# Nine unread products of ones around the transposes of the first tile's second norm, in a two-layer recurrent kernel

## Chip, cores and metric

One Trainium2 chip, one core. The metric is the device time of the kernel in microseconds (us). Most executions of a kernel agree within 0.3%. The engines are called by their short names: PE (TensorE: PE its products, PEld its weight loads), DVE (VectorE), ACT (ScalarE), POOL (GpSimd) and SP (SyncE, whose queue issues nearly all DMAs).

## What is computed

32 sequences of 256 tokens with 128 features go through two layers. Each layer normalizes its input, computes a recurrent branch `s` and a gate branch `g`, and adds `s * g`:

```python
x = L0_attn_x                                   # (32, 256, 128)
xn = _layernorm(x, axis=-1)
s = _L0_attn_ref(xn, ...)                       # k, v, r; decayed sums of exp(k) and exp(k)*v; sigmoid(r); Wo
g = _silu(_L0_ffn_ref(xn, ...))                 # three products with matrices of +1 and -1, relu between
x = x + s * g
xn = _layernorm(x, axis=-1)                     # the second norm
s = _L1_attn_ref(xn, ...)                       # W_in, causal conv of 4, silu, W_x, W_dt, softplus, a scan, W_out
g = _silu(_L1_ffn_ref(xn, ...))                 # 2 shared and 16 routed experts, the 4 likeliest, gelu
x = x + s * g
```

## The kernel before

The tokens are cut into 16 tiles of 512 (two sequences), numbered 0 to 15. Most of a tile's arrays are 128 features x 512 tokens. A product that must be exact in float32 is made of three products of rounded parts ("h" for the high part, "l" for the low one: w_h by x_h, w_l by x_h, w_h by x_l, the helper `mm3`, recorded at L634); each moves 512 columns. The products of seven of the nine expert groups (`pm<-act,w_n`) and the transposes are in plain float32.

Each stage of a tile is a Python generator that issues one instruction per step: `norm0`, `part0`, `mix`, `sign0` to `sign2` (tiles pha, phb, pz), `key`, `kv`, `recept` (pk, pv, pr), the sums, `quot`, `back` (po, and the transposes pt back to tokens x features), `norm1` (psb), `conv`, `proj`, `logits`, `router`, `gates`, `res`, `decay`, `gain`, `scan`, `outp`, `up`, `weigh`, `down`, `gate1`, `end`. What stands between two generators' steps is set by hand over the whole kernel: `ORDER` is a text of three-character entries, a tile and a stage, and the instruction that the stage issues next is put there. So every engine's queue is a part of one written list, and each engine works through its own part in that order. `SLOTS` names, for each buffer a stage asks for, which of the pool's places it gets; "psq" is the eight PSUM banks.

The place of the change is the second norm of tile 0. `norm1` takes statistics of the four 128-token pieces of `pt` on DVE (bsb, mvb: L659, L664), the inverse root on POOL (mvb, L669), normalizes each piece on DVE into `xnb` (L952, one 128x128 instruction per piece), and transposes each on PE into one bank `psb` (L956). ACT then copies the bank to x20h (L959, rounded) and DVE takes the rest x20l. All that follows in the second layer reads these two: the products pi and pres (`conv`, `res`), pl (`logits`, eight products of 32 columns, then DVE's reduction L1027) and pu (`up`, nine groups). The router goes on with an exponential of lg on ACT, and further reductions on DVE.

ACT evaluates its functions from tables. The helper `act` issues a table load (L410) where the function at hand isn't in the set that was loaded last. A kind "G" is the set with gelu, "S" the one with silu, "E" the one with exp and ln, "P" softplus. `tr` (tanh, in `recept`) is in "S" and in "G", and loads "S" where neither is there.

Products of ones are in the kernel already: `warm` (L493, L498) fills `wm`, 128x256, with ones, and issues WARM = 14 products `wm[:, 0:P]` by `wm` of 256 columns into a bank that nobody reads, 10 of them ahead of everything else on PE and four among the first products.

Of the kernel before, what the change touches and what calls it, by code (L numbers as in the profile page):

```python
# [16 lines left out]
P = 128  # L17
# [34 lines left out]
WARM = 14  # L52
WV = (1,)
# [54 lines left out]
        '0123045678250312530171120573663507222367502257603220367566275301132570002713511573207735201330152711'  # L108
        '357206635027117026535263170'
# [6 lines left out]
        '0123401221043210301243011043210424013240043210433104231001324103031423011023410220143201120341021204'  # L116
        '3120102341022103421001243103'
    ),
    'h': (
        '012341056789abc5147603ac167459b82def9f2d5fe89417cb6a30gd48ac84d7g23b9f51915fb193604827gdca4cag8c54d7'  # L120
        '2063bf9171736190afb42d8g5cb8b248c5gd71a963f07d63d7g849b25c0fa1b99c5b48d3f6g71a02a20172ag639fd85c4be4'
        'f3c53f90ga21674ff47624fa8b19g05c3e1b1c5b2697f48ae30gdb3d0ed345g8f679c18c96cba817f05dg416'
# [9 lines left out]
        '0123410532610762151760432154257262016421360403546030127013755147531650250435453743502615376542325635'  # L132
        '5753521073136243242133567061627674711474103462732241025402151603761476713733521354075716274030762700'
        '4561460135170171251324756562403123012105370657246247120643475127161340041041556237265737431704011604'
        '2056241673213723576060417245472522043734110723756356236247104323156315753653271534161721672027526342'
        '6405161501767261530175276374267743035134723640622474501664673701272140251706307130235045041507620543'
        '7316236723023754745104604303663025467375102130252312413657025302164301037637441270463527141026134571'
        '0012572743160732457347563'
    ),
    'rest': '0000000000000000',  # L140
    'rs': '01101010101010100101100110010110',
# [3 lines left out]
        '0120201210331200456721389046509183462920504382631594807461390470825a23481018973273991307128628531064'  # L145
        'a15037951a05430697341a87260489a3b0b63649623b0961257a3498c6892a756c68657a60b836a79543a584b890a3589c20'
        'b7240b5373b025053b78a504a2b580738b403a7283c9c4a09538c4537907c389405a6943ca2b65c4539b6935c2ab53c9b738'
        'a4c9057ba9874830b4a97b33b0296875920b657b989075a842b7653c1616c518474b42714812b0220021847b58451058501b'
# [4 lines left out]
    'xi': '01101010011001100110011010010110',  # L153
    'xna': '00',
    'xr': '0123454012354012',
# [5 lines left out]
g0pg0pg0pg0pg0p000g0hg0fg0pg0fg0fg0fg0fg00g0fg07g08g01100g0pg03002002002g0pg0fg0fg0gg0gg0hg04002g0og0o002g0g002002002g0g  # L161
g0g002g0ig0i002002002102102102g0jg0j102102102102102102g02g0gg0ag09g0cg0fg0fg0fg0m002g0k002002g0b002002102002002200002g0q
g0f102004g0fg0mg0d003008005102g0q102004102g0j003g0l005008004g0eg0kg0og05g0kg0fg0f102004102102006006102102102005300g0vg06
005007007008g0j00800e00e00e10100g00g00600g00e009006g0j00e00900900700700e00f00fg0j10300i00i00i00i00a00a00a00a00a00a00900a
00a00a10300900900900920220220220220220210510500g201g0v00f20220200b00b00b00b00900900h301g0l40100140000cg0t00cg0t20200c00c
00c00c00c20200c00j10600h106g0u00j00b00a00b00b00b00h202g0l00j00bg0r00b00j10820220200cg0u00cg0r10510510710720200d00dg0tg0t
g0t108g0sg0t109109106202302g0s10700j00d00d00d30210400j10c00d30210810c00d30250030230230230230210400j00d00k30200j00l00l109
10600l40210a30210c40220200l00l10c30210730210910430210a10410a10910810cg0ng0n10910c50240210e10e40270040240240240230200l00l
00l50240210c00m00l00m10c10c10e00m00m00m00m00m00m00m10i10i10e00m10910910a50250260040210a50250250250210a10a10a10e00m50210e
10a00m00m00m00m00m00m00m00m00n10f10f20210i109g0n50200m10f20400n00o20300n30210j10900q00n00q10c00q00q00q00q00q00o00q01s01s  # L170
01s10j60200q00n20360200o01k60201k00q60201k80060260200q60260201100r01s10j60201101101860210i00r00n01801800r00r00r30201k00n
01o01c00r00r01c70201o00r00r10a01100r01801c01o01470200r01410g01100r10g01o00r00r01gg0ng0n10g00o01110b01c01400r00r00n00o01g
01g70200u70200r10g10b01410b70270270270270200u00r01g90000u70210b00o00t00t10h00t10d01510b00n01901d00o10b00n10b10h00n10b10d
10d10d01l00u01p01w00o10b01001w10h01w01000o00o00o10b01001001030310d10d01601310d10d10j00t10j00p01601h01630401a00p00p10k00p
01301380201e01701720620680200p10j01080201t01780210j01x00p01ma0001b20610j10l10l20401q10l10l00s00z00z00z00s00s00w01f00w10l
00v20420820601i00v00z00z10l00z00y00y10l10l01u20880210l80280280201w10m10m20701j20700y10m20710m20520500x00x10m10m10m20501n
01y10m10m01020801r01v20701020801z10m20502040201020i20410m20i20e20940240280290200x80210m10m40220920e90210m10m20i20i10m10m
20e90210m40220920e10m20c90220910m902902902902209209c0010o10n20e10o10n00z90220c902a0210n00za02a02a0220e00z10q10qb0010q10q
10q10q30320f10q20f10q20f10o10n20950102120910o20a20a20c40210o20a02110n10q10q10q10n20j10r20j02102120c40220c20c20c10r10r20c
02102120c20a11802120a20911820j40311802111811120c11111111c10r20911c11c11c40411k10r10o10r10r20a40311k02111o11o11k10r11o10r  # L180
11k10r10o20a20a10r11o10r11g11110r11g11g10r11s10r10n11g11s11s10r10o11411411120g20g10r20g20a11111410r11s20b10n11420b20b115
20g10t20b11d20b20a20b20b20h11310n10n10n20b11911320h20b11l10t10t10u10u10u20h20b20d20d20d20d20d11610o10o10z10z10z10o11311t
10t11p20j11e10p11620j10u11w10p10p20j10p20d20d11w20d10p11611h20j11a11x11w20k11711711011020j20l20l20l10p11m11711w20l305305
30810s11b30530420l10s10s10z10w308305110110110a02a02a02a0211q10w30420l10v10y10y11i10v20l20l20l30e11f30820m30e20m30630610y
10x10x10z11y11010z50230811j50250230620m11u110502307307307a0230611n50220m20m20m20m20m20m11011r30720m11011vb0230420mb02b02
b0211z10x120a0220m20m30id0030i30930i30920m20m60120m20m20m30i30e30930e30a30a10z30e40410z10z30e30f30f20m50230c40430a30f30a
30930930c30930930c30c30c30930c12150230930c30c12120n20m12112120n30j12112130c20n30920o30c30j20o20n20o30a12120n20q20q20q20q
20q20q20q12120q21120o20q21121120q30j20o30a20q21k30a30a20n20r20r20r20r21k12140421o21o21k21s20r21c21k20o21s21s21o21121c21c
20o21s21g21c20r21g20r21820r20r20n20r21821121821420r21821420r20r21g20r21421130a30g30g21g30g20r21o30b30a20r30b30b20o20r214
30b30b30g30b20r21w21321w30b20n30h21321320o20o20t21520t20t30h20o21w21d20n20n30b30d30h20n21930d21l20t30d30d30j21t30j21030b  # L190
21030b30j20u50450330d20u20u21021021030d30d30j21630d21e21020u21h30j30l30l21630k40640621a21p30l30l40620z21x20z20z21640620p
21720p20p20p21720z20z30l20p21721b21m30l20p21i30l30l21u20s30l30m30m20w30m30m21f21j20s20s20w21q30m30m30m30m30m20y20y20v405
40520v21n21r30mc02c02405c0240521w40720y20x40760220x21y21v602602407b02602b02b02b02408c0240i40i20z210e0040821z40i407b02b02
21030m22060221040i20x40e70140930m30m40e40e30m30m30m30m40930m20z40840c40940e50430m30m20z20z40a40a40e40e60240c40c409408409
40940c40940c40c22122160240c40f40f40c40f40a40940c40a30o40922130o50422122122130n22150440j40a30n40j30n40940c30n30q30q30q221
30q30q30q30q30q30o40a40a30q30n40a30q30q30o30r40j30n30r30r30r31850322131c31c31831831c31131831131130n31k30o30r31o31o31o31c
31130r30r31k31k31k30r30r30n30r31s31s31s30r30r31430r30r31430o31431131g31o31g30r31g31131s40g40g40a30r40g30r30o31w31w31g40a
30r31w31440b40b40g40b40b31530o40b40b40b30t30n30n40b31d30n30t31331930t31l31330o30o40h30o31p31340d40h40d40d40d40b40h40j30u
30t30u40b30u60330p31630p30p31h40j40j31630p50650630p40d40d31e40d31731640d40j31730u31031040j40k31a31t31x40l40l60430p40l40l
31050631031050631m30z30z31740l30s30z30v30s30s30w31i31b30w30vc02c02c02c0240l30y30y30z30z31f40l40l31w40m31u40m70240l30z702  # L200
# [96 lines left out]
def recurrent_d2(  # L297
# [634 lines left out]
    def norm1(i):  # L932
# [3 lines left out]
        if N1 == "b" and i not in N1D:  # L936
            yield from spread(s, "xn2", mv, f"b{i}", lambda: s["r"], "back", E1)
            yield
            nc.scalar.copy(hi_of(s, "x2", f"x2{i}", "x2"), s["xn2"])
            yield  # L940
            lo_of(s, "x2", f"x2{i}", "x2", s["xn2"], E1[2])
            return
        for j in range(NJ):
            yield
            if j == 0:
# [437 lines left out]
```

## Time and profile before

| what | value |
|---|---|
| median of 3 runs | 659.92 us (659.65, 659.92, 661.74) |
| the profiled execution, its own time | 659.82 us |
| its span from the first to the last instruction | 658.0 us |
| mean granted clock of PE over the span | 0.993 |
| ACT's table loads (L410) | 99, 127.0 us in all, 1283 ns each |
| the transposes of the second norms (L956) | 64, in tile 0 from 39.54 us |

The page gives each engine's busy time, cuts the span in 40 slices of 16.45 us, and follows back the chain of work that ended last. Timelines give start, duration, engine, line, operation, tiles, and in brackets the idle time before with what ended it. A busy PE is not PE at its peak, since products overlap: how far apart they begin says more than how long each lasts. Times in a timeline or window are us from the start of the span.

### The profile page before, as it was taken

How to read it: one execution, taken by the hardware profiler on the slowest of the kernel's cores; microseconds unless marked ns; L12 is line 12 of the kernel's file. 1: busy time of each engine (PE TensorE's matmuls, PEld its weight loads, DVE VectorE, ACT ScalarE, POOL GpSimd, SP SyncE). 2: the span in 40 equal slices, each digit the busy share in tenths (PEclk: the TensorE clock that was granted, in tenths of full speed). 3: DMA queues.
4: the chain of work that ended last, by engine and by line, in shares of the span. 5: the costliest groups of instructions: out<-in, count | busy, mean ns of one | idle time of the engine just before them, and what ended most of it. 6: DMA issues, size and time to landing. Idle time of an engine off the chain costs nothing.

```text
span 658.0 us, 8819 instructions
## 1 busy us (share of the span) xinstructions
PE 641.4 (97%) x2626; PEld 461.5 (70%) x2626; DVE 572.2 (87%) x1364; ACT 549.3 (83%) x911; POOL 384.0 (58%) x398
## 2 busy tenths in 40 slices
PE   8999999999999999999999999999999999999997
PEld 6667676876757777576777767677675876767664
DVE  5989999979988899888888988988888798979886
ACT  8969797878969879797888979889797997967984
POOL 6585848567392773828466393944738374262542
PEclk9979999999999999999999999999999999999999
DMA  7334223142230413204132220413123040310431
GB/s 239 138 80 142 69 84 113 64 130 65 93 103 32 137 59 114 65 24 144 43 132 65 87 91 30 133 49 130 47 71 110 17 130 12 91 46 0 146 94 69
DMA packets 43648, 57.38 MB, mean 87 GB/s; under 512 B 3936, under 2 KB 20432, under 8 KB 43600
## 3 DMA queue, kind: packets, MB, share of 16 engines
q1 hardware_dynamic: 43456, 56.80, 26.9%
q8 instruction: 21, 0.34, 0.2%
q14 instruction: 27, 0.22, 0.1%
q10 hardware_dynamic: 144, 0.01, 0.0%
HBM read 52.02 MB, written 4.78 MB: 86 GB/s over the span
## 4 chain that ended last, share of the span: by engine, by line
PE 78%; DVE 11%; ACT 6%; issue 2%; DMA 2%; POOL 1%; SPq 0%; DVEq 0%; ACTq 0%
PE phb L634 15%; PE pm L634 14%; PE pu L634 13%; PE pc L634 6%; PE pha L634 4%; PE pz L634 3%; PE pi L634 3%; PE py L634 3%; PE pres L634 3%; PE pp L634 2%; PE po L634 2%; PE pk L634 2%; PE pl L634 2%; PE pv L634 1%; ACT L410 1%
## 5 line engine op out<-in xcount | busy, mean ns | idle before, releaser
L414 POOL TENSOR_TENSOR act<-act,ge 128x512 f32<-128x512 f32 x109 | 139.2, 1301 | 19.3 <-DMA ge<-gd 14.7
L410 ACT ACT_TABLE_LOAD x99 | 127.0, 1283 | 2.8 <-PEq L1371 1.2
L634 PE MATMUL pm<-act,w_n 128*128 128x512 f32 x224 | 106.0, 592 | 0.0
L417 DVE SCALAR_TENSOR_TENSOR pi<-xiz,par_sb,pi 128x512 f32<-128x512 f32 x96 | 70.4, 744 | 1.0 <-ACT pi L976 0.7
L414 POOL TENSOR_TENSOR xc_0l<-y,xc_0h 128x512 fp32r<-128x512 f32 x15 | 19.4, 1296 | 85.0 <-ACT y L411 64.3
L634 PEld LDWEIGHTS pm<-act,w_n 128*128 128x128 f32 x224 | 41.8, 189 | 29.9 <-issue 23.5
L411 ACT ACTIVATE act<-pu 128x512 f32<-128x512 f32 x109 | 61.2, 601 | 1.2 <-PE pu L634 0.3
L414 POOL TENSOR_TENSOR y<-y,rs 128x512 f32<-128x512 f32 x30 | 38.3, 1278 | 18.7 <-DVE y L1122 18.1
L1122 DVE TENSOR_TENSOR_SCAN y<-pd,y 128x256 f32<-128x256 f32 x64 | 39.9, 669 | 4.4 <-ACT pd L411 4.1
L414 POOL TENSOR_TENSOR xr<-gm,xr 128x512 f32<-128x512 f32 x15 | 19.3, 1288 | 30.1 <-DVE gm L414 25.1
L634 PE MATMUL phb<-ha_0h,w 128*128 128x512 f32 x64 | 27.3, 431 | 0.1
L1056 POOL MEMSET m<- 128x16 f32 x16 | 1.8, 112 | 43.7 <-DVE m L1054 43.7
L634 PE MATMUL phb<-ha_0l,w 128*128 128x512 f32 x64 | 26.1, 410 | 0.0
L634 PE MATMUL phb<-ha_2h,w 128*128 128x512 f32 x64 | 25.6, 403 | 0.0
L634 PE MATMUL phb<-ha_1h,w 128*128 128x512 f32 x64 | 25.5, 401 | 0.0
L634 PE MATMUL phb<-ha_3h,w 128*128 128x512 f32 x64 | 25.5, 398 | 0.0
L411 ACT ACTIVATE pd<-pd 128x512 f32<-128x512 f32 x32 | 17.9, 581 | 9.0 <-PE pd L634 8.8
L634 PE MATMUL phb<-ha_3l,w 128*128 128x512 f32 x64 | 25.3, 396 | 0.0
L634 PE MATMUL phb<-ha_2l,w 128*128 128x512 f32 x64 | 25.2, 397 | 0.0
L952 DVE TENSOR_SCALAR xnb<-pt,mvb 128x128 f32<-128x128 f32 x64 | 22.8, 401 | 2.3 <-POOL mvb L669 2.2
L634 PE MATMUL phb<-ha_1l,w 128*128 128x512 f32 x64 | 24.7, 396 | 0.0
L414 POOL TENSOR_TENSOR xc_1l<-y,xc_1h 128x512 fp32r<-128x512 f32 x15 | 19.4, 1296 | 8.7 <-ACT y L411 8.7
(1160 smaller groups left out, 2201.9 us busy)
## 6 DMA issues: line engine op xcount, KB each, us to landing
ge<-gd SPq DMA_DIRECT2D x128, 256.0 KB
mra<-mda SPq DMA_DIRECT2D x28, 256.0 KB
xt<-in_x SPq DMA_DIRECT2D x16, 256.0 KB
xr<-in_xr SPq DMA_DIRECT2D x16, 256.0 KB
out_x<-xr SPq DMA_DIRECT2D x16, 256.0 KB
w_up<-in_w_up SPq DMA_DIRECT2D x3, 192.0 KB
gd<-gT SPq DMA_DIRECT2D x16, 32.0 KB
w_n<-in_w_down SPq DMA_DIRECT2D x1, 448.0 KB
```

Of the source, the lines that this page charges most:

```text
L410: nc.scalar.preload_act_table_set(SETS[kinds[0]])
L411: nc.scalar.activation(*args, **kw)
L414: getattr(nc, engine).tensor_tensor(o, a, b, op)
L417: nc.vector.scalar_tensor_tensor(o, a, s, b, op0, op1)
L634: nc.tensor.matmul(ps, lhsT=w, rhs=r, start=start, stop=stop)
L952: nc.vector.tensor_scalar(xn[:, j, :], s["pt"][:, j, :], mv[:, j, 0:1], r, ALU.subtract, ALU.mult)
L1056: nc.gpsimd.memset(m8[:, :, TOPK:8], -1.0)
L1122: nc.vector.tensor_tensor_scan(y[:, tok], sp[:, tok], y[:, tok], 0.0, ALU.mult, ALU.add)
```

## The change

A setting WARM2 = 6 comes in. For tile 0 alone, `norm1` issues six products of ones (128x128 by 128x128, plain float32) into the last quarter of psb's bank ahead of the transposes, and one after each of the first three transposes, nine in all. The fourth transpose overwrites that quarter; the products are not read. The bank is taken at the first product, no longer at the first transpose.

```diff
+WARM2 = 6
...
+        for k in range(WARM2 if i == 0 else 0):
+            yield
+            if k == 0:
+                ps = bank([P, NJ, P], f"psb{i}", "psn")
+            mm(ps[:, NJ - 1, :], wm[:, 0:P], wm[:, 0:P])
         for j in range(NJ):
             yield
...
             yield
-            if j == 0:
+            if j == 0 and not (WARM2 and i == 0):
                 ps = bank([P, NJ, P], f"psb{i}", "psn")
             nc.tensor.transpose(ps[:, j, :], xn[:, j, :], ident)
+            if WARM2 and i == 0 and j < NJ - 1:
+                yield
+                mm(ps[:, NJ - 1, :], wm[:, 0:P], wm[:, 0:P])
```

`ORDER` and the strings of `SLOTS` are made anew as a whole, from 5244 steps to 5253, so nearly every line of them differs. Apart from the nine products and one table load (100, not 99) each engine has the same instructions as before, in another order. Around the place of the change the new order reads:

- PE: phb ..., one product of ones, five phb products, two of ones, one phb, three of ones, then transpose, ones, transpose, ones, transpose, ones, transpose, then pi (h by h), pi (l by h), pi of the second half (h by h), pr, pi (h by l), the eight pl, pi, pi, pu. Before: phb ..., four transposes, pi, pr, pi, pi, pi, seven pl, pi, pl, pu. The set of PE's other products ahead of the first transpose is the same in both.
- DVE: xnb, xnb, a half scan wkz, xnb, xnb, a half scan, pk, x20l. Before: four xnb, two half scans, x20l, pk.
- ACT, after x20h: x12h, r, t1z, xiz, r, pi, lg, table load, tr, table load, act (gelu of pu), and on with gelus. Before: hb, t1z, x12h, r, xiz, r, pi, lg, table load, act, tr, act.
- In the first 39 us: ACT's casts of w_o and of the first third of w_u, which stood ahead of r0's logarithm, stand after it, the cast of w_y stands later, and that of w_c behind g0; POOL's low part of w_c is later too; DVE's g0 comes two instructions earlier; the weights' loads and the tiles' loads change places in SP's queue.

## The prediction

> **What bounds the kernel now.** I read the page first, then busy time by window along the steps of the clock, then the order of events on TensorE (PE), the chain of waits, and ScalarE (ACT) and VectorE (DVE) around the place of the change.
>
> ```profile
> span 658.0 us, 8819 instructions
> PE 641.4 (97%) x2626; PEld 461.5 (70%) x2626; DVE 572.2 (87%) x1364; ACT 549.3 (83%) x911; POOL 384.0 (58%) x398
> PEclk9979999999999999999999999999999999999999
> ```
>
> PE is busy nearly all the time and is 78% of the chain of waits, so PE's clock is time. One slice in 40 has a lower clock, the fourth. Windows of 3.41 us laid on its edges (PE's busy time and products begun, then the granted clock):
>
> ```profile
> 24.61:28.03 3.42, 2.50 (x10) 1.00 0.01 4
> 28.03:31.44 3.41, 2.76 (x11) 1.00 0.56 156
> ...
> 38.27:41.68 3.41, 2.38 (x9) 1.00 0.47 132
> 41.68:45.09 3.41, 3.41 (x13) 0.50 0.00 0
> 45.09:48.51 3.42, 3.42 (x10) 0.50 0.15 25
> 48.51:51.92 3.41, 3.41 (x16) 1.00 0.14 52
> ```
>
> The clock is half for two windows exactly, behind the window with the least PE work of all that lie ahead of it; a window of 2.50 us did not bring it down. What made that window thin, on PE:
>
> ```profile
> 38.79 0.40 PE L634 MATMUL phb<-ha_3l,w 128*128 128x512 f32 x1
> 39.54 1.28 PE L956 MATMUL psb<-ident,xnb 128*128 128x128 f32 x4 [0.35 <-DVE xnb L952]
> 41.50 0.67 PE L634 MATMUL pi<-x20h,w_i_h 128*128 128x512 f32 x1 [0.68 <-ACT x20h L959]
> ```
>
> Between 39.02 (38.79 plus the 0.233 us at which 512-column products follow each other) and 41.50 PE has only the four transposes of tile 0's second norm. After it, products begin 0.428 us apart instead of 0.233. Half a clock for 6.83 us is 3.41 us of PE's work lost.
>
> But PE is not alone there. DVE waits for PE once, at the router's reduction, and from there to 63.35 us the chain of waits runs on DVE; ACT has no idle time worth naming from 47.15 to 63.17. First three pieces of the chain, then the timelines of DVE and ACT:
>
> ```profile
> 45.83 0.02 issue
> 45.85 0.29 DVE lg L1027
> ...
> 63.37 0.59 ACT z1h L897
> ```
>
> ```profile
> 45.85 0.29 DVE L1027 TENSOR_REDUCE lg<-pl 128x64 f32<-128x128 f32 x1 [1.61 <-PE pl L634]
> 47.15 0.26 ACT L411 ACTIVATE lg<-lg 128x64 f32<-128x64 f32 x1 [1.48 <-DVE lg L1032]
> 47.42 1.28 ACT L410 ACT_TABLE_LOAD   x1
> 48.72 0.60 ACT L411 ACTIVATE act<-pu 128x512 f32<-128x512 f32 x1
> 49.21 0.59 ACT L411 ACTIVATE tr<-pr 128x512 f32<-128x512 f32 x1
> ```
>
> **The change, part by part.** *Nine products, on PE.* They are 128 columns wide. The warm-up products L498 (128x256, two passes each: 28 rows for 14) begin 0.216 us apart a pass once the clock is up; the 32-column router products (pl) of later tiles, 0.112 us. Half of the first is 0.108, below the second, so I take 0.112 a pass, 0.224 a product, 2.0 us for nine; the upper bound is 0.216 a pass, 3.9 us. PE's other work ahead of the transposes is the same set in both orders. Six products (1.34 us) stand ahead of the first transpose, in a gap of 0.52 us (39.02 to 39.54): it moves to 40.36, 0.82 late. Before, the transposes are 0.32 apart, DVE's pace; with a product between them 0.224 + 0.035 (the pace of transposes back to back) = 0.26. So the last begins at 41.14, not 40.49: 0.65 late. The new order also puts a half scan (wkz, 0.6 us) between the second and third of DVE's four xnb; the fourth is then done by 39.07 + 4 x 0.34 + 0.6 = 41.03, in time. ACT's copy x20h and the first pi product follow at their old distance: pi at 42.15. Bounds of this term: nothing, if the rest of the order makes the room, and 2.5 us at the upper price (six 2.6, then 0.47 apart). Nothing reads the products, and the bank they use is freed without a wait; it is taken earlier, but its next user is the router's, as before.
>
> *The clock.* Do products of ones keep it up? At the start PE ran nothing else from 1.19 to 7.21 us, and their passes go from 0.427 us apart to 0.216 at 4.2 us: they count. With them, PE in the stretch that was thin works all but the 0.7 us for x20h and the transposes, about 2.4 us of each 3.41, against some 1.2 now (three products and a part of pi at 0.233, transposes at 0.035 to 0.1). The window of 24.61, some 1.8 by the same count (seven products and the rest of one), was enough. So the half clock goes. PE does from 42.15 in 0.18 + 3.41 us what it had done by 48.51: it is there at 45.74, 2.77 ahead. Bounds: 0 (clock falls anyway) and 3.41 (products free).
>
> A rule speaks against this. The Trainium skill ("TensorE: Matmul & The Clock Gate", sections "Part 1: The HAM clock gate" and "HAM oscillation") lets the clock halve only after an idle window of about 3.4 us. By that rule no such gap existed, the nine products could save nothing, and the sum would be the costs alone, about 661.8 us. The row decides: 0.35 and 0.68 us of idle time were enough here. The same page ("Part 4: PE-mode transpose") says transposes do not count as busy in the same way, which would explain the row; that the window runs free, as Part 1 says, no single profile can show.
>
> *What DVE gets of it.* From pi to the reduction the new order has five 512-column and eight 32-column products: 42.15 + 5 x 0.233 + 8 x 0.112 + 0.2 = 44.4, so 1.45 ahead of 45.85. DVE's own work before it (x20l, two hb lows, one statistic, 2.1 us after x20h at 42.1) ends about then too.
>
> *One more table load on ACT.* 100 loads instead of 99, 1.28 us each. It stands here: after lg the new order has load, tr, load, then the first gelu; before it was load, gelu, tr. ACT reaches lg 1.45 ahead, and the third activation after it only 0.17 ahead. With no idle time it stays so until z1h, where it waits 0.20 for DVE; next it has 1.2 and 1.4 us to spare (66.97 and 72.00). DVE needs ACT's results in between: z1l at 64.48 could start at 63.96 - 0.17 - 0.20 = 63.59, 0.9 ahead. Price on the path: between nothing (DVE's and PE's other work goes ahead) and 1.28.
>
> *The rest of the order.* The first 39 us are reordered: ACT does r0 without the w_o and first w_u casts ahead of it (0.74 us of rows), DVE's waits of 0.31 (e) and 0.32 (g) can shrink: I take 0.3 us gained, bounds -0.3 and 0.6. In it, too, stands that SP's first loads change places (k0 earlier, w_x ahead of tile 2's input) while the DMA engines are 0.86 busy (10 to 20 us). Later, the counts of instructions are equal, and so is the closeness of work to what it waits for: PE instructions with at most two of PE's own between them and their latest foreign producer are 71 before and 73 after, DVE's 453 and 458. PE's listed waits after 100 us are 5.2 us; I take no change, with 2 us either way.
>
> *Sum.* With the load paid in full: 0.9 + 0.3 = 1.2 us gained. With PE's lead kept: 2.77 + 0.3 = 3.07. The chain is on DVE to 68.5 and on PE after it, so neither row is nearer and I take the middle, 2.1. The profiled execution took 659.82 (span 658.0 and 1.8 around it), 0.1 below the median of the three runs, so no correction: 659.82 - 2.1 = 657.7 us.
>
> **The rivals.** *The clock falls all the same, or in the next thin window* (slower). Place: the windows around 24.61 to 31.44 with 2.50 and 2.76 us, little above the 2.38 that fell, or the 0.7 us still open before pi. For it: the threshold lies between two near numbers. Against: products that took PE's clock up at the start, and twice the work in the window. It decides as soon as the window holds less than about half PE work. Then the 0.65 and the 1.28 are paid for nothing: 661.8, with dearer products (2.5) 663.6; middle 662.7.
>
> *The lead is swallowed* (no change). DVE is busy 10.00 of 10 us from 50 to 60, ACT 9.83, and ACT's lead is 0.17. If later tiles' stalls stay where they are, 0 to 0.9 is left: 658.9 to 659.8, middle 659.4. Against it: ACT's spare time after 64 us.
>
> *Not what it says*: the 128-column products do not count as the 256-column ones did. This gives the first rival's time; no row speaks for it.
>
> **How the numbers follow.** What can be told from no change is about 0.3%, 2.0 us: below 657.9 is faster, above 661.9 slower. Forecast 0.68, its own range 656.1 to 659.0 (656.75 and 658.6 are the two ends of the sum, widened by 0.65 and 0.4 for the order), of which 0.45 faster and 0.23 within. Clock falls: 0.18, of which 0.17 slower, 0.01 within. Swallowed: 0.14, of which 0.11 within, 0.02 slower by stalls elsewhere, 0.01 faster. Together 0.46 faster, 0.35 within, 0.19 slower. Range for 8 in 10: down to 656.0 (3.07 and 0.75 of the 2 us of the order), up to 662.7, the middle of the slower rival, so that its upper half and what lies under 656.0 are left out.
>
> **What would show it.** The fourth slice of the clock row at full; products 0.233 apart behind pi; last transpose near 41.1, pi near 42.1, the reduction near 44.4; two table loads around tr and the first gelu not before 49.0; z1l 0.9 us or more earlier than 64.48. Wrong if any stretch of half clock remains before the last microseconds, if the transposes are over 2 us late, or if PE's waits after 100 us differ by more than 2 us from 5.2.

## The result and the profile after

The changed kernel takes 663.01 us (median of 20 executions, 661.21 to 664.85), the kernel before 660.38 us beside it (20 executions). The ratio is 1.0037, with a 95% interval of 1.0025 to 1.0049: slower by 2.4 us, where 2.1 us of gain were forecast. The profiled execution took 661.66 us.

The head of the page of the changed kernel (span, busy time of each engine, granted clock in 40 slices):

```profile
span 659.9 us, 8847 instructions
PE 640.9 (97%) x2644; PEld 460.6 (70%) x2644; DVE 571.9 (87%) x1364; ACT 549.6 (83%) x912; POOL 384.8 (58%) x398
...
PEclk9999999999999999999999999999999999999999
```

The 7 in the fourth slice is gone and the clock is full throughout, as forecast; the span is 1.9 us longer all the same. PE's timeline around the transposes, in the changed kernel:

```profile
40.88 0.61 PE L635 MATMUL psb<-wm 128*128 128x128 f32 x4
41.24 0.48 PE L635 MATMUL phb<-ha_3l,w 128*128 128x512 f32 x1
41.56 0.83 PE L635 MATMUL psb<-wm 128*128 128x128 f32 x6
42.22 0.27 PE L963 MATMUL psb<-ident,xnb 128*128 128x128 f32 x1
...
43.23 0.27 PE L963 MATMUL psb<-ident,xnb 128*128 128x128 f32 x1
44.18 0.50 PE L635 MATMUL pi<-x20h,w_i_h 128*128 128x512 f32 x1 [0.68 <-ACT x20h L969]
```

A product of ones shows as two passes, 0.112 us apart. The fourth transpose stands at 43.23 and pi at 44.18; the prediction had 41.14 and 42.15. So a pass is as dear as forecast, but all stands 2.0 to 2.1 us later than forecast. What DVE and ACT do next, in the changed kernel:

```profile
46.48 0.29 DVE L1037 TENSOR_REDUCE lg<-pl 128x64 f32<-128x128 f32 x1
```

```profile
48.00 0.26 ACT L412 ACTIVATE lg<-lg 128x64 f32<-128x64 f32 x1 [0.46 <-DVE lg L1042]
48.27 1.28 ACT L411 ACT_TABLE_LOAD   x1
49.57 0.60 ACT L412 ACTIVATE tr<-pr 128x512 f32<-128x512 f32 x1
50.18 1.28 ACT L411 ACT_TABLE_LOAD   x1
51.48 0.60 ACT L412 ACTIVATE act<-pu 128x512 f32<-128x512 f32 x1
...
65.43 0.59 ACT L898 CAST z1h<-pv 128x512 fp32r<-128x512 f32 x1
```

The reduction is 0.63 us later than before (45.85), not 1.45 earlier. The second load is paid too: the first gelu is 2.76 us later (48.72 before), z1h 2.06 us (63.37 before).

When the same instruction begins, against the profile of before, tells where the 1.9 us came in: z0h (ACT, 30.45 before) +1.85, x20h (40.86) +2.68, the reduction +0.63, z1h +2.06. ACT's z0h and x20h, in the kernel before and then in the changed one:

```profile
30.45 0.56 ACT L897 CAST z0h<-pv 128x512 fp32r<-128x512 f32 x1
40.86 0.59 ACT L959 CAST x20h<-psb 128x512 fp32r<-128x512 f32 x1 [0.46 <-PE psb L956]
```

```profile
32.30 0.58 ACT L898 CAST z0h<-pv 128x512 fp32r<-128x512 f32 x1
43.54 0.59 ACT L969 CAST x20h<-psb 128x512 fp32r<-128x512 f32 x1 [0.70 <-PE psb L963]
```

So 1.85 us are lost before the products begin.

### The profile page after: what moved, and what is told of

It reads as the page before. It is cut to its first block, busy times and chain, and to the rows that moved or that the text cites. A ratio compares the mean times of both kernels' runs of the same rounds, so it can differ in the third digit from the quotient of the medians.

```text
span 659.9 us, 8847 instructions
## 1 busy us (share of the span) xinstructions
PE 640.9 (97%) x2644; PEld 460.6 (70%) x2644; DVE 571.9 (87%) x1364; ACT 549.6 (83%) x912; POOL 384.8 (58%) x398
## 4 chain that ended last, share of the span: by engine, by line
PE 69%; ACT 9%; DVE 8%; POOL 5%; DMA 4%; issue 3%; SPq 1%; POOLq 0%; DVEq 0%; ACTq 0%
PE pm L635 15%; PE phb L635 13%; PE pu L635 10%; PE pc L635 5%; PE pha L635 4%; PE pz L635 3%; PE py L635 3%; PE pres L635 3%; PE pi L635 2%; ACT L411 2%; DMA ge<-gd 2%; POOL act L415 2%; PE pp L635 2%; ACT act L412 2%; PE po L635 2%
## 5 line engine op out<-in xcount | busy, mean ns | idle before, releaser
L986 ACT ACTIVATE pi<-pi,par_sb 128x512 f32<-128x512 f32 x32 | 23.9, 751 | 0.5
```

Of the source, the lines that this page charges most:

```text
L986: nc.scalar.activation(pi, pi, AF.Identity, bias=col(CONVB + h), scale=col(cw + 3))
```

## The experiments

Ratios are against runs of the kernel before on the same chip, with 95% intervals; "z0h at" is its start against before's 30.45. Edits of the written order are shown one step a line: tile, stage, what it issues.

**Without the extra table load.**

```diff
  0 router  lg (exp, ACT)
- 1 recept  tr (tanh, ACT)
...
  0 up7     act (the first gelu, ACT)
+ 1 recept  tr
```

> The changed kernel with one step moved: tr of tile 1 (tanh) goes behind the first gelu of tile 0, so that ACT has 99 table loads again. Theory A (three costs: 1.85 us in the first 30 us from the new order, 0.8 us from the products, 1.4 us from the extra load near 50 us, against 2.05 us gained from the clock): the first gelu starts 1.2 us or more earlier than in the changed kernel (51.5), z1h comes 1.3 us earlier than its 65.4, and the time falls by 0.7 to 1.4 us against the changed kernel (663.0 with before at 660.4), to about 661.9. Rival B (the later part of the new order is worse, the load is absorbed): z1h earlier, but the time within 0.4 us of 663.0.

661.22 us, ratio 1.0005 (0.9996 to 1.0014), z0h at +1.69, z1h at +0.55. The load costs 0.0032 of 660, 2.1 us, more than the 0.7 to 1.4 of Theory A. The start's loss stays.

**Before's order with the nine products.**

```diff
+ 0 norm1   six products of ones (PE)
  0 norm1   xnb (DVE)
...
  0 norm1   transpose (PE)
+ 0 norm1   a product of ones     (after each of the first three)
```

> The order of before with the nine products put in by hand: six directly ahead of the first transpose, one behind each of the first three. Theory A: no half clock behind the transposes, pi of tile 0 0.7 to 0.9 us late, the router's reduction 1.2 to 1.5 us earlier than 45.85, and the time 0.8 to 1.6 us below before (about 659.2). Rival B (the lead is swallowed by DVE and ACT in any order): within 0.4 us of before. Rival C (the products themselves are what costs): 0.5 us or more above before.

660.47 us, ratio 0.9995 (0.9981 to 1.0010). In its profile x20h loses 0.79 us against z0h (+0.24, then +1.03), the reduction is 0.68 us and z1h 0.65 us earlier than before, and nothing of it is seen in the median: Theory A by its profile, Rival B by its time. So the change without its new order is worth nothing that can be measured here (the interval runs from 1.3 us gained to 0.7 lost). One of its twelve executions has a mean clock of 0.996, the others 0.998 or more.

**The new order without the nine products.**

```diff
-WARM2 = 6
+WARM2 = 0
...
- 0 norm1   the nine products of ones (PE)
```

> The new order with the nine products taken out. Theory A: the half clock of two windows is back behind the transposes, the 1.85 us of the start and the 1.4 us of the load stay: about 663.5 to 664.5, so the products help the new order by 0.5 to 1.5 us. Rival C (the products cost more than they bring): 662.5 or less, below the changed kernel.

663.82 us, ratio 1.0045 (1.0032 to 1.0058): 0.5 us above the changed kernel, as Theory A has it, but the intervals overlap. The half clock of two windows is back, from 45.10 to 51.93 us, and three of its six executions have a mean clock of 0.992 or 0.993. z0h is at +1.98, so the products don't make the start late; nor does the clock's phase, for the clock goes up at 4.14 us here, as in the profile before (4.13), and at 6.54 in the changed kernel. Its fourth transpose is at 43.28, where the changed kernel has 43.23: the half scan between DVE's xnb all but hides the products there.

**Before's start, then the new order, with the products.**

```diff
- the new order's first 442 steps
+ before's first 433 steps, with the nine products in their places
  the new order from its step 442 on
```

> The order of before with the nine products up to the step behind tr of tile 1 (the first 433 of its steps), from there on the new order. So the start is the old one and the extra table load is gone; all that follows is new. Theory A: 659.0 to 659.8 with before at 660.4, as with the old order and the products. Rival B (the later part of the new order costs): 661.5 or more.

659.54 us, ratio 0.9979 (0.9969 to 0.9989), with 99 loads: Theory A. With the first steps as they were and no second load, what is left of the change is a gain, of 1.4 us. The next run asks whether the products have a part in it.

**The same without the products.**

```diff
-WARM2 = 6
+WARM2 = 0
```

> This is the kernel of the run before-start-then-new (ratio 0.9979) without its nine products of ones. Theory A, the products keep TensorE's clock and this is worth something once the order around them costs nothing: a stretch of half clock of 6.8 us stands again at about 41 to 49 us, x20h comes about 0.8 us earlier than in that run (1.25 - 0.45 = 0.8 us was lost there between z0h and x20h), and the time is 0.5 to 2 us above it: 660.5 to 661.5 us, ratio 0.9995 to 1.001. Theory B, the gain of that run is the later order alone and the clock is worth nothing, since VectorE bounds the stretch: half clock again, but a ratio of 0.997 to 0.9985. If it is at or below 0.997, the products cost more than the clock they keep.

659.18 us, ratio 0.9980 (0.9966 to 0.9994): Theory B by its time. But its profile shows no half clock between 5.48 and 657.42 us, against both theories, though nothing had been added to the thin stretch. Its windows, laid on the edge at which the clock went up (us, busy time and count of PE, PEld, DVE, ACT, POOL, then granted clock, DMA share, GB/s):

```profile
36.20:39.61 3.41, 3.23 (x14) 2.07 (x13) 2.80 (x17) 2.30 (x3) 2.83 (x7) 1.00 0.76 223
39.61:43.02 3.41, 2.41 (x9) 1.50 (x10) 3.41 (x8) 2.94 (x7) 3.25 (x5) 1.00 0.22 77
43.02:46.44 3.42, 3.42 (x21) 2.88 (x19) 3.42 (x15) 3.10 (x7) 3.02 (x4) 1.00 0.00 0
```

The window begins 1.34 us later than before's (39.61 against 38.27), the thin stretch only 0.4 us later: the window's end now takes in what follows the stretch, and the clock holds. This is one execution: three of the run's twelve have a mean clock of 0.994 or 0.995, nine 0.998 or more. So the question became how often the clock falls at all. The mean granted clock of each execution tells it: a fall of two windows costs 3.41 of 658 us, 0.005. Of the 77 executions of the kernel before that stand beside these runs (one disturbed one left out) 29 have 0.995 or less, 45 have 0.998 or more, 3 lie between.

**Before with the extra load alone.**

```diff
+ 1 recept  tr (tanh, ACT)
  0 up7     act (the first gelu, ACT)
...
- 1 recept  tr
```

> The kernel before, with one change: ScalarE's second recept activation of tile 1 stands ahead of the first gelu, so that there are 100 table loads of 1.28 us instead of 99, and no product of ones. Theory A, the load is paid in full and nothing of it is made good later: 1.3 to 2.1 us longer, ratio 1.002 to 1.0032, and z1h 0.9 to 1.5 us later than before's 63.37. Theory B, the midpoint of the prediction, half of it: about 0.65 us, ratio 1.001. Theory C, hidden, because with the half clock TensorE is late here anyway: ratio 0.999 to 1.0005.

662.68 us, ratio 1.0028 (1.0012 to 1.0044), z1h at +0.90: Theory A, paid in full. Of its ten executions only two have a mean clock of 0.998 or more.

**The two places at the start.** ACT's first work of tile 0, in the kernel before and then in the changed one:

```profile
4.27 0.39 ACT L584 CAST w_d<-w_dt 128x256 fp32r<-128x256 f32 x1
4.69 0.51 ACT L590 ACTIVATE hi_d<-w_d,par_sb 128x256 f32<-128x256 f32 x1
...
6.16 0.72 ACT L515 ACTIVATE w<-w0t,sgn 128x512 fp32r<-128x512 f32 x1 [0.78 <-DVE w0t L513]
...
6.88 1.63 ACT L719 ACTIVATE xna<-xt,ofa,mva 128x128 f32<-128x128 f32 x4
...
9.52 0.58 ACT L732 CAST x10h<-psa 128x512 fp32r<-128x512 f32 x1
```

```profile
6.43 0.72 ACT L516 ACTIVATE w<-w0t,sgn 128x512 fp32r<-128x512 f32 x1 [1.95 <-DVE w0t L514]
7.05 0.39 ACT L585 CAST w_d<-w_dt 128x256 fp32r<-128x256 f32 x1
7.54 0.51 ACT L591 ACTIVATE hi_d<-w_d,par_sb 128x256 f32<-128x256 f32 x1
7.95 1.63 ACT L720 ACTIVATE xna<-xt,ofa,mva 128x128 f32<-128x128 f32 x4
...
10.00 0.69 ACT L753 ACTIVATE t1z<-psa,omm 128x512 f32<-128x512 f32 x1
11.51 0.59 ACT L733 CAST x10h<-psa 128x512 fp32r<-128x512 f32 x1 [0.82 <-DVE xm L418]
```

First, w_d and hi_d stood in ACT's wait for w0t and now stand behind it, ahead of xna, which begins 1.07 us later (0.27 of this is w itself, behind a later w0t). Second, x10h waits 0.82 us for DVE's xm. Both read the bank psa, and in the kernel before it is the other way round, which DVE's row there tells:

```profile
10.19 0.75 DVE L417 SCALAR_TENSOR_TENSOR xm<-psa,par_sb,t1z 128x512 f32<-128x512 f32 x1 [2.63 <-ACT x10h L732]
```

By these rows the two readers go one after the other, in the order of the list, and ACT, which goes on to the other tiles, is now the one that waits. Three runs, all without the extra load, undo these one by one. The casts moved back:

```diff
  lam_b (ACT)
+ w_d  w_d (ACT)
+ w_d  hi_d (ACT)
...
  w0   w (ACT, behind DVE's w0t)
...
- w_d  w_d
- w_d  hi_d
...
-        hi_d = wt([P, 256], "hi_d", "tmp")
+        hi_d = wt([P, 256], "hi_d", "hid")
```

> The changed kernel without its extra table load (the run no-extra-load, ratio 1.0005, z0h at +1.69), and with ScalarE's two casts w_d and hi_d moved ahead of w0, as the kernel before has them. Theory A, these two casts are 0.9 to 1.07 us of the loss at the start, since ScalarE waits for w0's load ahead of them and has no idle time from 10 to 30 us: the first normalised block 0.8 to 1.0 us earlier, z0h at +0.7 to +0.9, and a time of 660.2 to 660.7 us, ratio 0.999. Theory B, the other loss (the VectorE step of the first mix behind ScalarE's copy x10h) takes the place of it: z0h stays at +1.6 and the ratio at 1.0005.

660.50 us, ratio 1.0003 (0.9988 to 1.0017), z0h at +1.13: the profile moves 0.56 us of Theory A's way, little more than z0h moves by itself between executions (see the end), and the time not at all. xna begins at 7.22 there, behind a wait of 1.07 us for POOL's ofa, so it was not the casts alone that kept it from its old 6.88. Then the copy moved ahead of xm:

```diff
+ 0 part0   x10h (ACT)
  0 mix     xm (DVE)
- 0 part0   x10h
```

> The changed kernel without its extra table load, and with tile 0's copy x10h ahead of the VectorE step of the first mix; the casts w_d and hi_d stay where the change put them. With the runs no-extra-load (neither mended, 1.0005), casts-first (1.0003) and start-mended (both, 0.9971) this is the fourth corner. Theory A, the copy is the whole of it and the casts cost nothing by themselves: 0.997 to 0.998, z0h at +0.2 or less. Theory B, the two places only work together, since ScalarE has no idle time behind the casts and each delay covers the other: 0.9995 to 1.0005, z0h at +0.9 to +1.6. In between (0.9985 to 0.9995, z0h at +0.6 to +0.9) each is half of it.

659.30 us, ratio 0.9977 (0.9963 to 0.9990): with two neighbours of the list exchanged, 0.0028 or 1.85 us are back against the run without the load. No engine's own order changes by this, only which of the two waits for the other. z0h is at +0.39, so it is Theory A by its time and nearly so by its profile. ACT in it:

```profile
7.83 1.63 ACT L766 ACTIVATE xna<-xt,ofa,mva 128x128 f32<-128x128 f32 x4
9.36 0.49 ACT L533 CAST w_k_h<-wkvro 128x384 fp32r<-128x384 f32 x1
9.88 0.69 ACT L799 ACTIVATE t1z<-psa,omm 128x512 f32<-128x512 f32 x1
10.46 0.58 ACT L779 CAST x10h<-psa 128x512 fp32r<-128x512 f32 x1
```

xna is still 0.95 us later than before, but x10h begins 0.58 us after t1z with no wait; in the changed kernel it is 1.51 us (10.00 to 11.51). And both:

```diff
  lam_b (ACT)
+ w_d  w_d, hi_d (ACT)
...
- w_d  w_d, hi_d
...
+ 0 part0   x10h (ACT)
  0 mix     xm (DVE)
- 0 part0   x10h
```

> The changed kernel without its extra table load, with the two casts ahead of w0 as in the run beside it, and with the copy x10h of tile 0 ahead of the VectorE step of the first mix, so that the two readers of that PSUM bank come in the order of the kernel before. Theory A, these two places are the whole of the 1.85 us lost at the start: z0h within 0.3 us of before's 30.45, lg 0.5 to 1 us ahead of before's 45.85, a time of 659 to 660 us, ratio 0.997 to 0.9985, as the run before-start-then-new has it. Theory B, the loss has other places too (the order of SyncE's first loads, VectorE's first scans): z0h at +0.6 or more and a ratio of 0.999 to 1.0005.

658.91 us, ratio 0.9971 (0.9958 to 0.9984), z0h at -0.16: Theory A, and the reduction is 1.38 us earlier than before, more than it gave. This is the best version found, faster than both kernels. Of the two places, the copy is nearly all: the casts' part is 0.0002 without the copy mended and 0.0006 with it, within what these runs can tell from nothing.

**Where the load's other 0.8 us go.** The load alone is 1.28 us, 2.1 were measured. Of the changed kernel's 20 executions nine have a mean clock of 0.998 or more and take 662.27 us in the mean, eleven have 0.996 or 0.997 and take 663.75. Without the load and with the products (the run without the load, before's start then new, the three just above, and before's order with the products) 70 of 71 have 0.998 or more; the other is the one with 0.996 in before's order. The nine executions above are in the mean 1.6 us over the kernel before beside them, those without the load 0.3 us: 1.3 us apart (standard error 0.5), which is the load's length. So the changed kernel ran twice more, and before once:

> The changed kernel as it is, for one more execution with its profile. In 11 of its 20 executions the mean granted clock is 0.996 or 0.997, and these are 1.5 us longer than the other nine (663.75 against 662.27); the profile at hand is of one with 0.999. In all 12 executions without the extra table load it is 0.998 or more. Theory A, the load empties a window of TensorE around 49 to 52.4 us (an idle wait of 1.42 us for the gelu behind the load), and where a window of the clock's grid falls on it the clock is halved for one window of 3.4 us: an execution with a mean clock of 0.997 shows half clock that begins at 51.5 to 54 us. Theory B, it is the thin stretch at 460 to 467 us that the runs without the load have too: half clock there. Theory C, only the end of the kernel, where the half clock begins up to 5 us before the last instruction: no record of half clock in between.

663.16 us, clock 0.998, no half clock but at the end (Theory C's row, but for an execution without the fall).

> The same kernel and question as in the run beside it, for another phase of the clock's windows against the kernel: half clock that begins at 51.5 to 54 us if the mean clock is 0.996 or 0.997 (Theory A), around 464 to 470 us (Theory B), none but at the end (Theory C).

662.86 us, clock 0.997, and Theory A. Windows, then PE's timeline, of this execution:

```profile
45.96:49.37 3.41, 3.41 (x18) 2.62 (x18) 3.41 (x15) 2.92 (x5) 3.25 (x7) 1.00 0.19 64
49.37:52.79 3.42, 1.75 (x7) 0.91 (x6) 3.12 (x20) 3.38 (x6) 1.98 (x5) 1.00 0.04 13
52.79:56.20 3.41, 3.41 (x10) 2.64 (x9) 1.11 (x3) 3.25 (x7) 0.00 (x0) 0.50 0.00 0
56.20:59.61 3.41, 3.41 (x17) 2.71 (x16) 3.41 (x11) 2.46 (x5) 1.24 (x2) 1.00 0.07 22
```

```profile
50.24 0.51 PE L635 MATMUL pu<-x20h,w_u_h 128*128 128x512 f32 x1 [0.27 <-ACT tr L412]
52.15 0.50 PE L635 MATMUL pu<-x20h,w_u_h 128*128 128x512 f32 x1 [1.41 <-ACT act L412]
```

PE waits 0.27 and 1.41 us for tr and act, the activations behind the two loads. That empties a window (1.75 us of busy time), and the clock is halved for the next: the very loss that the nine products were to prevent, ten microseconds on.

> The kernel before as it is, for another execution with its profile. In 24 of its 62 executions the mean granted clock is 0.995 or less, in 36 it is 0.998 or more; the first are 0.84 us longer in the mean. Theory A, whether the clock falls at the transposes is a matter of where the clock's free-running windows of 3.41 us lie against the kernel: with a release r at the start the grid is r + n x 3.41, and the clock falls only where a whole window of it begins between about 38.0 and 39.3 us. So a profile with a release at about 4.7 to 6.8 us (or 3.41 us earlier) shows no half clock in between, one at 3.9 to 4.7 us shows it from 41.4 to 42.2 us on for 6.83 us. Theory B, it falls in every execution and the mean clock differs by the ends alone.

662.21 us; the clock went up at 4.195 us, and its windows follow that edge:

```profile
38.33:41.74 3.41, 2.38 (x9) 1.12 (x9) 3.22 (x13) 2.93 (x6) 3.25 (x5) 1.00 0.34 117
41.74:45.15 3.41, 3.41 (x13) 2.93 (x12) 2.56 (x5) 3.17 (x7) 3.41 (x4) 0.50 0.00 0
45.15:48.57 3.42, 3.42 (x10) 2.74 (x10) 2.67 (x13) 1.92 (x3) 1.38 (x3) 0.50 0.10 37
```

Half clock from 41.74 for 6.83 us: the row that Theory A gives for a release between 3.9 and 4.7 us. With 0.994 it is one of the executions that fall, so the other half of Theory A rests on the run without products (the clock goes up at 5.48 us, no fall) and on the clocks of the 77. The two other profiles without products fall as well, and the clock goes up early in both: at 4.14 us (new order without products) and at 4.54 (before with the load).

## Why the prediction was wrong

**The bound on the clock.** Wrong in how often, right in how. The prediction took the one profile for all executions: half clock in each, 3.41 us of PE's work. It stands in 29 of 77, and these take 661.41 us in the mean against 660.40 for the 45 without it: 1.0 us (standard error 0.22), and 29/77 of it, 0.4 us, in the mean of all. That is what a held clock can gain by these runs, where the forecast counted 2.77 us of lead in every execution. That DVE bounds much of the stretch would explain why 3.41 us of PE's work are only 1.0 us of time; it was not tried by itself.

**Products of ones keep the clock.** Right: 70 of 71 executions with the products and without the extra load have a clock of 0.998 or more; without the products and without the load, 29 of 77 and 3 of 12 have 0.995 or less. The rival in which the clock falls all the same was in the right place with its time (661.8 to 663.6 us), but by luck, not by its mechanism: the clock does fall in 11 of 20, but where a profile shows it, by the load's stall and not in the windows the rival named.

**Their price.** Right: 0.112 us a pass, 0.79 us at x20h in before's order (0.65 forecast). One part was too low: transposes with a product between them were taken to be 0.26 us apart and are 0.33 (42.22, 42.56, 42.89, 43.23). As far as the intervals tell, the products' price and what the clock brings cancel: ratios 0.9979 with and 0.9980 without them, the rest alike.

**The first 39 us, "0.3 us gained, bounds -0.3 and 0.6".** The step that failed first: 1.85 us are lost at z0h, and mending the two places gives back 0.0034 of the time, 2.2 us (0.0028 or 1.85 us by the copy alone). The term was priced by the casts that left the path and two waits of DVE, and by nothing that came onto the path. The exchange of x10h and xm, one place in the list, wasn't seen; the row of before with xm waiting for x10h shows what it would do. The fourth xnb, forecast for "41.03, in time", ends at 43.11 and fell with it.

**The extra table load, between nothing and 1.28 us, the middle taken.** Mis-sized: 2.1 us. 1.28 of it is the load in full (1.3 us are left in the executions without a fall); that ACT's lead of 0.17 us was gone with the start is the likely reason. 11/20 x 1.48 = 0.81 is the half clock that its stall brings, if the whole difference between the two groups is put down to it. The sum is 2.09; the half clock wasn't in the forecast at all.

**PE's lead of 2.77 us, the reduction at 44.4.** Right where the start is in time and the second load is gone: in the best version the fourth transpose is at 41.23, pi at 42.18 and the reduction at 44.47 (forecast 41.14, 42.15, 44.4), and its ratio of 0.9971 is near the forecast's (657.7 / 659.92 = 0.9966). That is luck in part and not the clock's doing: before's start with the new order and no products has 0.9980 too.

**The rest of the order, "no change, with 2 us either way".** Within its bounds: that same run puts the later order at 1.3 us gained (interval 0.4 to 2.2), the clock's part of it included. Which steps of it gain wasn't tried. PE's waits after 100 us are 6.6 us, 5.2 before.

**The swallowed lead.** Right for before's order: there the reduction and z1h came 0.7 us earlier and the median did not move (0.9995).

The sum by the measured sizes, from 660.4: products and clock 0, the start +1.85, the load +2.1, the later order -1.3, makes 663.0 us; 663.01 were measured. That it meets so closely is luck, for each term is known to about 1 us only, and the load's was itself taken from the changed kernel's time.

## What to carry to other kernels

A loss that one profile shows may be there in a part of the executions only: read the clock of every run before pricing it, and lay the windows on the edge at which the clock went up. Where an order is made anew, compare it instruction by instruction for two readers of one buffer that change places and for work that stood in an engine's wait and no longer does; such a pair of neighbours cost more here than the change could gain. A stall of another engine that empties a window of TensorE is to be priced with the half clock behind it.

## What the runs showed of the hardware

The clock's windows are 3.41 us long and not tied to the kernel: the clock went up at 4.13 to 6.97 us after the first instruction, and every later edge is a whole number of windows behind (before: 41.67 - 4.13 = 11 x 3.413). The Trainium skill ("TensorE: Matmul & The Clock Gate", section "Part 1: The HAM clock gate") says so, 3413 ns and free-running; here the records agree. Its other rule, that an idle window lets the clock fall, is too mild for these runs: the clock fell behind windows that were not idle. Recorded busy time doesn't tell which: windows with 2.38 us (before), 2.11 (new order without products) and 1.75 (the changed kernel's third time) fell, one with 2.41 (before's start without products) and one with 2.02 (the changed kernel once more, from 607.72 us) did not. Counting PE's work instead, a 512-column product as 0.233 us, a 256-column pass of ones as 0.216 and a transpose as 0.035, the windows that fell held 0.85 us (new order without products), 0.97 (before with the load), 1.07 (before once more), 1.08 (before) and 1.21 (the changed kernel's third time); the least that stayed held 1.15 (new order without products, from 7.55 us) and 1.16 (the one of 2.41). So an estimate of the limit is a third of a window; by this count it is no sharper. Whether a transpose counts at all these runs don't tell, since four of them are only 0.14 us of a window. The fall lasted two windows at the transposes and one behind the load; why was not tried.

The same steps begin up to 0.45 us apart from one execution to another at z0h with before's start (30.45 to 30.90) and 0.55 with the new one (31.88 to 32.43). Further on they wander more: between the two profiles of the kernel before, the same product of PE is 0.1 us apart at z0h, 2.6 at 300 us and 1.7 at 550; between the first two of the changed kernel the sign changes, from 1.0 us later at 400 to 0.4 earlier at 500. One profile's end tells less than a median of twelve.
